# Reordered exponentials in a cross-attention loop, and a regrouped last expert stage

## The chip, the cores and the metric

One core of one Trainium2 chip runs one program: a two-layer decoder with every array in float32. The metric is the device time of one launch in microseconds (us), as the median of several launches. The kernel before takes 1028.84 us (three launches, 1027.73 to 1029.24).

## The reference, cut to what matters

The decoder works on 8 batches of 256 tokens with 128 features. The change lies in the last two of its six blocks, the second layer's cross attention and its mixture of experts:

```python
def _L1_xattn_ref(input_Q, input_K, input_V, Wq, bq, Wk, bk, Wv, bv, Wo):
    Q = _proj(input_Q, Wq, bq)          # 16 heads of 64 features
    K = _proj(input_K, Wk, bk)          # 512 positions of memory
    V = _proj(input_V, Wv, bv)
    scores = jnp.einsum('bhqd,bhkd->bhqk', Q, K) / np.sqrt(DK).astype(np.float32)
    attn = jax.nn.softmax(scores, axis=-1)
    context = jnp.einsum('bhqk,bhkd->bhqd', attn, V)
    ...
    return jnp.einsum('bse,de->bsd', context, Wo)

def _L1_ffn_ref(x, Wr, br, W1, b1, W2, b2):
    cap = max(1, int(T / E * CAPACITY_FACTOR))     # 40 slots for each of 8 experts and each batch
    ...                                            # top 2 experts of each token, buf holds the kept tokens
    h = jax.nn.relu(jnp.einsum('enc,ech->enh', buf, W1) + b1[:, None, :])
    y = jnp.einsum('enh,ehc->enc', h, W2) + b2[:, None, :]
    ...                                            # weighted sum of each token's two results
x = _layernorm(x + _L1_xattn_ref(x, ctx_1024, ctx_1024, ...), axis=-1)
x = _layernorm(x + _L1_ffn_ref(x, ...), axis=-1)
```

## The kernel before

**The loop.** Keys and values of the cross attention are computed early in the launch, kept in DRAM and loaded again. `cross_attention` then walks 64 units: a unit is one batch b and one pair of heads c (8 batches, 8 pairs). A unit has two blocks j of 128 queries, and each block two heads h. Every step i of the loop works at three units at once: it scores unit i+1, turns the weights of unit i, and multiplies the weights of unit i-1 with the values.

**The order.** The whole loop is recorded under a manual schedule. TensorE, VectorE, ScalarE and SyncE each execute their instructions in the order in which `step` issues them; an instruction whose input or buffer isn't ready holds all that stands behind it on its engine. So the order of calls in `step` is the order of work on each engine. In one step that is, by engine:

- TensorE: `score` of the next unit, block 0 and then block 1 (tile `sc`, four instructions each, L400); `product` of the former unit (tile `m`, L400); `query` of the next batch (tile `tr`, L400); the transposes of `turn(now, 0)` and then those of `turn(now, 1)` (L1508).
- ScalarE: the exponentials of `weigh(after, got, j, h)` (L1494, one 128x512 instruction each, which also sums); `keep` (L1533), which empties the product's bank; `ask` (L357), which empties the query's bank; copies of turned weights (L1605, L1613). Before the change the order is: exponential (0,0), (0,1), `keep`, `ask`, exponential (1,0), copy of `turn 0`, exponential (1,1), two copies of `turn 1`.
- VectorE: two maxima (L1487), `divide(now, 1)` (L351, L353), a copy of `turn 0` (L1604), `divide(after, 0)`.

**The buffers.** PSUM has three groups of buffers here: `sc` with 2 buffers of two banks (block 0 and block 1 of a unit's scores), `tr` with 3, `m` with 1. A buffer is handed out in turn, and its next writer waits for the last reader of the former content. A plain step takes four `tr` buffers, in this order: the query, two for `turn 0`, one for `turn 1`. With three to hand out, the one for `turn 1` is the buffer that held this step's query, so the transposes of `turn 1` wait until `ask` has read it; its other half goes to `m`, which `keep` empties. The scores of block 1 of the next unit wait until the exponentials (1,0) and (1,1) of the unit before have read theirs.

**Beside the loop.** When a batch ends (`before[1] == NQ - 1`), `finish` projects the batch on TensorE (64 matmuls into `tr`) and normalises it on VectorE. `LastExperts.route` then chooses the experts of that batch's tokens in ten pieces, which are spread over later steps; piece 0 takes a `tr` buffer and a ScalarE copy (`xr`, L1650), piece 1 a small matmul and the exponential `prob` (L1664), piece 5 a small matmul (`pos`), piece 7 the dispatch (`bufT`, L1719).

**The last stage.** `LastExperts.rest` runs behind the loop. The 8 experts run first over batches 0 to 4 (`GROUPS[0]`, 200 columns) and then over batches 5 to 7 (`GROUPS[1]`, 120 columns): `expert` makes the hidden layer (tile `sc`, then Relu on ScalarE, L1748), `result` the output (tile `tr`, then VectorE adds the bias into `val`, L1757); `settle` issues a `result` that is still pending. `back(b)` takes batch b's results back to its tokens: three transposes (L410), a ScalarE copy (L1791), and in `rest` 12 matmul instructions (L400), the sum `y` (L1799), the statistics and, one batch later, the normalised `X` (L1809) and the store. `come_back(b)` issues the transposes of batch b and then the rest of batch b-1. Before the change the transposes go to a `tr` buffer and the 12 matmuls to the one `m` buffer; two batches come back before the second group starts, three between its experts, and three behind it.

Of the kernel before, what the change touches and what calls it, by code (L numbers as in the profile page):

```python
# [21 lines left out]
P = 128  # L22
B, S, D = 8, 256, 128
SC = 512
# [119 lines left out]
class Decoder:  # L144
# [203 lines left out]
    def divide(self, u, j):  # L348
        nc, pr = self.nc, self.weights[u][j]
        rd = self.tile(self.small, [P, 2], "c_rd")  # L350
        nc.vector.reciprocal(rd, self.sums[u][j])  # L351
        for h in range(2):
            nc.vector.tensor_scalar_mul(pr[:, h, :], pr[:, h, :], rd[:, h : h + 1])  # L353
# [1088 lines left out]
    def cross_attention(self):  # L1442
# [6 lines left out]
        with self.space("ct", 2) as pool, self.space("cp", 2, space=PSUM) as ps:  # L1449
# [21 lines left out]
            def query(b, c):  # L1471

                pm = turned()
                self.mm_halves(pm[:, :S], self.wqT[:, P * c : P * (c + 1)], xTs[b])
                return pm

            def score(u):

                sc, nm = [], []
                for j in range(2):  # L1480
                    sc.append(self.tile(ps, [P, 2, SC], "sc"))
                    for h in range(2):
                        ch = slice(HD2 * h, HD2 * (h + 1))
                        self.mm(sc[j][:, h, :], queries[u][ch, P * j : P * (j + 1)], keys[u][ch, :])
                for j in range(2):
                    nm.append(self.tile(self.small, [P, 2], "c_nm"))
                    nc.vector.tensor_reduce(nm[j], sc[j], AX.X, ALU.max, negate=True)  # L1487
                prs[u] = [self.tile(self.big, [P, 2, SC], "pr", 4) for _ in range(2)]
                sums[u] = [self.tile(self.small, [P, 2], "c_sm") for _ in range(2)]
                return sc, nm  # L1490

            def weigh(u, got, j, h):
                sc, nm = got
                nc.scalar.activation(  # L1494
                    prs[u][j][:, h, :], sc[j][:, h, :], AF.Exp, bias=nm[j][:, h : h + 1],
                    accum_out=sums[u][j][:, h : h + 1],
                )
# [17 lines left out]
            def product(u):  # L1515

                b, c = u
                pc = pcs[u] = product_bank()[:, :S]
                prT = prTs.pop(u)
                for n in range(NC):  # L1520
                    for h in range(2):
                        at = P * c + HD2 * h
                        self.mm(
                            pc[HD2 * h : HD2 * (h + 1), :], vals[b][:, n, at : at + HD2], prT[:, NC * h + n, :],
                            n == 0, n == NC - 1,
                        )

            def keep(u):

                b, c = u  # L1530
                if c == 0:
                    cTs[b] = self.tile(pool, [P, NQ, S], "cT", 1)
                nc.scalar.activation(  # L1533
                    cTs[b][:, c, :], pcs.pop(u), AF.Identity, bias=self.cols[:, BV + c : BV + c + 1]
                )
# [27 lines left out]
            def step(i):  # L1563


                after, now, before = (units[k] if 0 <= k < len(units) else None for k in (i + 1, i, i - 1))
                b, c = now or (B, 0)
                got = score(after) if after and after not in early else None
                if before:
                    product(before)  # L1570
                if b + 1 < B:
                    for what in "kv":
                        self.recall(b + 1, c, what)
                    pm = query(b + 1, c)
                if c == 0 and now:
                    self.load_last_experts(b)
                if now and now not in early:
                    divide(now, 1)
                while late and i:
                    late.pop()()  # L1580
                if got:
                    weigh(after, got, 0, 0)
                    weigh(after, got, 0, 1)
                if before:
                    keep(before)
                if b + 1 < B:
                    self.ask(b + 1, c, pm)
                if before and before[1] == NQ - 1:
                    experts.early()
                    finish(before[0])  # L1590
                    routes[:] = routes[-1:] + [experts.route(before[0])]
                if now:
                    if routes and c:
                        next(routes[-1], None)
                    if len(routes) > 1:
                        for _ in range({2: 1, 5: 2}.get(c, 0)):
                            next(routes[0], None)
                    if c == 5 and b + 2 < B:
                        begin(b + 2)
                if got:  # L1600
                    weigh(after, got, 1, 0)
                if now:
                    one, two = turn(now, 0)
                    nc.vector.tensor_copy(*one)  # L1604
                    nc.scalar.copy(*two)  # L1605
                if got:
                    divide(after, 0)
                    weigh(after, got, 1, 1)
                while late:
                    late.pop()()  # L1610
                if now:
                    for what in turn(now, 1):
                        nc.scalar.copy(*what)  # L1613
# [11 lines left out]
class LastExperts:  # L1625
# [158 lines left out]
    def back(self, b):  # L1784

        nc, dec, X = self.nc, self.dec, self.X
        pt = self.tile(self.ps, [P, 4 * P], "tr", 3)[: self.CUT, : 3 * D].rearrange("p (n d) -> p n d", n=3)
        for n in range(3):
            dec.flip(pt[:, n, :], self.yT[:, b, self.CUT * n : self.CUT * (n + 1)])
        ys = self.tile(self.pool, [self.CUT, 3, D], "prT", 2)  # L1790
        nc.scalar.copy(ys, pt)  # L1791

        def rest():
            po = self.tile(self.ps, [P, SC], "m", 1)[:, : 2 * D].rearrange("p (j d) -> p j d", j=2)
            for j in range(2):
                for n in range(3):
                    dec.mm(po[:, j, :], self.backT[:, 2 * b + j, n, :], ys[:, n, :], n == 0, n == 2)
            y = self.tile(self.pool, [P, 2, D], "y")
            nc.vector.tensor_tensor(y, X[:, 2 * b : 2 * b + 2, :], po, ALU.add)  # L1799
            mv, rstd = dec.tile(dec.small, [P, NT, 2], "mv"), dec.tile(dec.small, [P, NT], "rstd")  # L1800
            for j in range(2):
                st = dec.tile(dec.small, [P, 6], "bnst")
                nc.vector.bn_stats(st, y[:, j, :])
                nc.vector.bn_aggr(mv[:, j, :], st)
            dec.rsqrt(rstd[:, :2], mv[:, :2, 1], 2, 1.0, 1e-5)

            def end():
                for j in range(2):
                    nc.vector.tensor_scalar(  # L1809
                        X[:, 2 * b + j, :], y[:, j, :], mv[:, j, 0:1], rstd[:, j : j + 1], ALU.subtract, ALU.mult  # L1810
                    )
                nc.sync.dma_start(
                    out=dec.out[b].rearrange("(j p) d -> p j d", p=P), in_=X[:, 2 * b : 2 * b + 2, :]
                )

            return end

        return rest

    def rest(self, former, route):  # L1820
        first, second = self.GROUPS
        rests, ends = [], []

        def go_on():
            ends.append(rests.pop(0)())
            if len(ends) > 1:
                ends.pop(0)()

        def come_back(b):
            rests.append(self.back(b))  # L1830
            if len(rests) > 1:
                go_on()

        self.run(first, 2)
        for piece in range(10):
            next(route, None)
            if piece in (0, 1, 3, 5):
                self.run(first)
            if piece in (1, 2, 3):
                next(former, None)  # L1840
        assert self.done == NE
        self.settle()
        for b in first[:2]:
            come_back(b)
        for n in range(NE):
            self.run(second)
            if n in (1, 3, 5):
                come_back(first[2 + n // 2])
        self.settle()
        for b in second:  # L1850
            come_back(b)
        go_on()
        ends.pop()()
# [81 lines left out]
```

## Time and profile before

| | us |
|---|---|
| median of three launches | 1028.84 |
| the profiled launch | 1028.9 |
| its span, first to last instruction | 1026.8 |
| outside the span | 2.1 |
| cross-attention loop, first to last `product` | 543.9 to 957.1 |
| last experts and ways back | about 955 to 1026.8 |
| granted TensorE clock in the loop, as a share of full speed | 1.00 |

Busy time over the whole span: TensorE 933.5 us (91%), VectorE 715.5 (70%), ScalarE 708.6 (69%), GpSimd 221.7 (22%). All times below are of the one profiled launch, counted from the start of its span. In a row of the timeline the first number is the start, the second the duration; brackets give the engine's idle time before the row and what ended it. PE is TensorE, DVE VectorE, ACT ScalarE, POOL GpSimd. A row of PE shows a matmul's modelled end; consecutive matmuls overlap, so the distance between starts tells more than the durations.

### The profile page before, as it was taken

To read this page: it belongs to the slowest core of one execution; us is meant where nothing else is said; L and a number is where in the kernel's file an instruction comes from. 1 tells how busy PE (TensorE), PEld (TensorE's weight loads), DVE (VectorE), ACT (ScalarE), POOL (GpSimd) and SP (SyncE) were. 2 spreads that over 40 slices of the span, in tenths; PEclk is the share of its full clock that TensorE was granted. 3 is DMA by queue.
4 is the path that set the end of the run, shared out by engine and by line. 5 is a ranking of instruction groups with operands and counts; after the bars stand their busy time and mean duration, and the time that the engine had idled before them with its cause. 6 is when DMAs were issued, how large, how long until landed. Compare 5 with 4: busy or idle time off the path is not lost.

```text
span 1026.8 us, 21615 instructions
## 1 busy us (share of the span) xinstructions
PE 933.5 (91%) x8141; PEld 590.9 (58%) x8141; DVE 715.5 (70%) x1726; ACT 708.6 (69%) x1682; POOL 221.7 (22%) x394
## 2 busy tenths in 40 slices
PE   6897889999888788999879999999999999999986
PEld 2343556665478455666545555555555555555886
DVE  3787765454339847677677788897979797989244
ACT  5887698787654444756557878787878787878442
POOL 1133232434225463336300000000000000010012
PEclk9998899999999989999899999999999999999998
DMA  6743565223773400000262232323232223300001
GB/s 225 232 159 93 187 201 165 91 109 147 270 233 104 161 17 25 9 6 12 14 234 80 83 104 70 101 73 114 73 99 88 94 83 104 98 8 2 2 6 37
DMA packets 84376, 103.08 MB, mean 100 GB/s; under 512 B 7200, under 2 KB 45224, under 8 KB 84272
## 3 DMA queue, kind: packets, MB, share of 16 engines
q1 hardware_dynamic: 79472, 96.68, 29.1%
q10 hardware_dynamic: 3776, 2.92, 0.9%
q0 software_dynamic: 1024, 2.10, 0.7%
q8 instruction: 64, 1.05, 0.4%
q14 instruction: 40, 0.33, 0.1%
HBM read 56.13 MB, written 45.55 MB: 99 GB/s over the span
## 4 chain that ended last, share of the span: by engine, by line
PE 58%; ACT 18%; DVE 14%; issue 4%; DMA 2%; POOL 2%; SPq 0%; POOLq 0%; DVEq 0%; ACTq 0%
PE sc L400 15%; PE bank L400 14%; PE m L400 11%; PE tr L400 9%; ACT pr L1494 5%; PE tr L410 3%; PE po L400 2%; PE tr L1508 2%; ACT prT L1605 2%; DVE c_nm L1487 1%; ACT cT L1533 1%; DVE nm L1385 1%; PE bank L410 1%; DVE ys L597 1%; DVE pr L353 1%
## 5 line engine op out<-in xcount | busy, mean ns | idle before, releaser
L1494 ACT ACTIVATE pr<-sc,c_nm 128x512 f32<-128x512 f32 x248 | 170.4, 690 | 39.9 <-DVE c_nm L1487 39.9
L1487 DVE TENSOR_REDUCE c_nm<-sc 128x2 f32<-128x1024 f32 x124 | 148.1, 1219 | 3.6 <-PE sc L400 2.0
L400 PE MATMUL sc<-kT,qT 64*128 64x512 f32 x512 | 142.5, 635 | 8.2 <-ACT pr L1494 6.9
L400 PE MATMUL m<-prT,val 128*64 128x256 f32 x1024 | 124.7, 386 | 1.9 <-ACT prT L1613 1.9
L353 DVE TENSOR_SCALAR pr<-pr,c_rd 128x512 f32<-128x512 f32 x256 | 115.1, 492 | 4.6
L400 PEld LDWEIGHTS m<-prT,val 128*64 128x64 f32 x1024 | 67.9, 137 | 77.3 <-ACT prT L1613 48.2
L1508 PE MATMUL tr<-cst,pr 64*128 64x64 f32 x1536 | 87.9, 229 | 7.6 <-ACT qT L357 5.1
L1508 PEld LDWEIGHTS tr<-cst,pr 64*128 64x128 f32 x1536 | 74.0, 139 | 30.5 <-DVE pr L353 8.8
L400 PE MATMUL bank<-wvT,ctxT 128*128 128x512 f32 x128 | 69.3, 624 | 10.5 <-DMA wvT<-in_wvT_dram 9.1
L400 PEld LDWEIGHTS sc<-kT,qT 64*128 64x128 f32 x512 | 41.0, 190 | 59.8 <-ACT pr L1494 56.1
L400 PE MATMUL bank<-ctxT,wkT 128*128 128x512 f32 x128 | 70.9, 637 | 3.2 <-ACT stage L565 1.7
L415 POOL TENSOR_SCALAR rsq<-mv 128x2 f32<-128x2 f32 (+2 forms) x57 | 13.1, 230 | 276.0 <-DVE mv L587 129.4
L1604 DVE COPY prT<-tr 128x512 f32<-128x512 f32 x64 | 43.9, 686 | 24.7 <-PE tr L1508 24.6
L1393 ACT ACTIVATE s<-sc,nm 128x128 f32<-128x128 f32 x128 | 36.6, 374 | 30.2 <-DVE s L1390 25.8
L1605 ACT COPY prT<-tr 128x512 f32<-128x512 f32 x64 | 37.6, 588 | 24.5 <-PE tr L1508 24.5
L565 ACT ACTIVATE stage<-bank,cols 128x512 f32<-128x512 f32 x57 | 39.3, 689 | 21.2 <-PE bank L400 14.7
L535 ACT COPY sT<-tr 128x512 f32<-128x512 f32 x58 | 33.5, 593 | 29.4 <-PE tr L410 29.1
L569 ACT COPY stage<-bank 128x512 f32<-128x512 f32 x58 | 33.8, 584 | 27.5 <-PE bank L400 13.3
L1385 DVE TENSOR_REDUCE nm<-sc 128x8 f32<-128x1024 f32 x32 | 39.0, 1218 | 18.9 <-PE sc L400 18.7
L1494 ACT ACTIVATION_READ_ACCUMULATOR pr<-sc,c_nm 128x1 f32 x248 | 50.3, 203 | 0.0
L416 POOL TENSOR_TENSOR rstd<-rsq,mhalf 128x2 f32<-128x2 f32 (+2 forms) x57 | 49.2, 864 | 4.8
L1508 PE MATMUL m<-cst,pr 64*128 64x64 f32 x512 | 44.7, 228 | 0.0
(366 smaller groups left out, 2031.4 us busy)
## 6 DMA issues: line engine op xcount, KB each, us to landing
mv<-stage SPq DMA_DIRECT2D x64, 256.0 KB, 2.2
mk<-stage SPq DMA_DIRECT2D x64, 256.0 KB, 2.1
kT<-mk SPq DMA_DIRECT2D x64, 256.0 KB, 2.7
val<-mv SPq DMA_DIRECT2D x64, 256.0 KB, 3.0
sorted_x<-zero SPq DMA_DIRECT2D x8, 1024.0 KB, 6.3
w<-in_m_w_dram SPq DMA_DIRECT2D x23, 256.0 KB, 2.9
f_w<-in_f_w_dram SPq DMA_DIRECT2D x16, 256.0 KB, 3.9
ctxN<-in_ctx_dram SPq DMA_DIRECT2D x8, 256.0 KB, 3.8
```

The lines of the kernel that those rows point to most:

```text
L353: nc.vector.tensor_scalar_mul(pr[:, h, :], pr[:, h, :], rd[:, h : h + 1])
L400: self.nc.tensor.matmul(out, lhsT=lhsT, rhs=rhs, start=start, stop=stop)
L410: self.nc.tensor.transpose(out, in_, self.ident)
L416: self.nc.gpsimd.tensor_tensor(out, t[:, :n], self.mhalf[:, :n], ALU.pow)
L565: nc.scalar.activation(t, pm, AF.Identity, bias=bias)
L1385: nc.vector.tensor_reduce(nm, sc, AX.X, ALU.max, negate=True)
L1393: nc.scalar.activation(s[:, 1, v, :], sc[:, 1, v, :], AF.Exp, bias=nm[:, 4 + v : 5 + v])
L1487: nc.vector.tensor_reduce(nm[j], sc[j], AX.X, ALU.max, negate=True)
L1494: nc.scalar.activation(prs[u][j][:, h, :], sc[j][:, h, :], AF.Exp, bias=nm[j][:, h : h + 1], accum_out=sums[u][j][:, h : h + 1],)
L1508: self.nc.tensor.transpose(pt[:, n, :], prs[u][j][own, n // NC, P * (n % NC) : P * (n % NC + 1)], self.ident[own, own])
L1604: nc.vector.tensor_copy(*one)
L1605: nc.scalar.copy(*two)
```

## The change

It has two parts.

1. In `step`, the exponential (1,0) of the next unit is issued directly behind (0,1), ahead of `keep` and `ask`; the exponential (1,1) takes the place that (1,0) had, ahead of `turn(now, 0)` and its copies. ScalarE's order becomes: (0,0), (0,1), (1,0), `keep`, `ask`, (1,1), copy of `turn 0`, two copies of `turn 1`. The orders of TensorE and VectorE stay as they were.
2. In `LastExperts`, the transposes of `back` move to the `m` buffer and its 12 matmuls to a `tr` buffer. In `rest`, the second group of experts starts directly behind the dispatch, before any batch has come back. Batches 0 to 3 come back between its experts (behind experts 1, 3, 5 and 7), batches 4 to 7 behind it.

```diff
                 if got:
                     weigh(after, got, 0, 0)
                     weigh(after, got, 0, 1)
+                    weigh(after, got, 1, 0)
                 if before:
                     keep(before)
...
                 if got:
-                    weigh(after, got, 1, 0)
+                    weigh(after, got, 1, 1)
                 if now:
                     one, two = turn(now, 0)
                     nc.vector.tensor_copy(*one)
                     nc.scalar.copy(*two)
                 if got:
                     divide(after, 0)
-                    weigh(after, got, 1, 1)
...
     def back(self, b):
-        pt = self.tile(self.ps, [P, 4 * P], "tr", 3)[: self.CUT, : 3 * D].rearrange("p (n d) -> p n d", n=3)
+        pt = self.tile(self.ps, [P, SC], "m", 1)[: self.CUT, : 3 * D].rearrange("p (n d) -> p n d", n=3)
...
         def rest():
-            po = self.tile(self.ps, [P, SC], "m", 1)[:, : 2 * D].rearrange("p (j d) -> p j d", j=2)
+            po = self.tile(self.ps, [P, 4 * P], "tr", 3)[:, : 2 * D].rearrange("p (j d) -> p j d", j=2)
...
-        self.settle()
-        for b in first[:2]:
-            come_back(b)
+        backs = list(first)
         for n in range(NE):
             self.run(second)
-            if n in (1, 3, 5):
-                come_back(first[2 + n // 2])
+            if n in (1, 3, 5, 7):
+                come_back(backs.pop(0))
         self.settle()
-        for b in second:
+        for b in [*backs, *second]:
             come_back(b)
```

## Prediction

> **What bounds the kernel now.** I read the page first: TensorE is busy for 91% of the span, and PEclk is 9 from the loop on, so the clock is not the matter.
>
> ```profile
> PE 933.5 (91%) x8141; PEld 590.9 (58%) x8141; DVE 715.5 (70%) x1726; ACT 708.6 (69%) x1682; POOL 221.7 (22%) x394
> ```
>
> Then the chain that ended last, in order of time, over one plain step of the loop:
>
> ```profile
> 560.38 1.13 PE sc L400 x4
> 561.51 1.90 PE m L400 x16
> 563.42 0.02 issue
> 563.44 0.46 ACT cT L1533
> 563.89 0.35 issue
> 564.24 0.31 ACT pr L1494
> 564.55 0.26 issue
> 564.82 0.20 ACT pr L1494
> 565.01 0.48 ACT prT L1605
> 565.49 0.69 ACT pr L1494 x2
> 566.18 0.04 issue
> 566.22 1.13 PE sc L400 x4
> ```
>
> The reader sees a ring of 5.84 us: scores of block 1, product, `keep`, `ask` (the 0.35 of issue), exponential (1,0), a copy, exponential (1,1), and then the next scores of block 1, whose buffer that exponential empties. The distance between products is 5.83 or 5.84 in 24 steps. Then the timeline, TensorE and ScalarE:
>
> ```profile
> 564.95 1.08 PE L400 MATMUL sc<-kT,qT 64*128 64x512 f32 x4
> 566.22 1.13 PE L400 MATMUL sc<-kT,qT 64*128 64x512 f32 x4 [0.19 <-ACT pr L1494]
> ...
> 598.20 0.71 PE L1508 MATMUL tr<-cst,pr 64*128 64x64 f32 x16 [0.84 <-ACT qT L357]
> ```
>
> ```profile
> 563.44 0.47 ACT L1533 ACTIVATE cT<-m,cols 128x256 f32<-128x256 f32 x1 [0.42 <-PE m L400]
> 563.87 0.48 ACT L357 ACTIVATE qT<-tr,bq 128x256 f32<-128x256 f32 x1
> ```
>
> The ring costs TensorE only 0.19 a step, so TensorE alone would need 5.65. The third row shows a second gate: transposes wait 0.84 for `ask` (qT), since they take the buffer that held the query. The waits, over the loop:
>
> ```profile
> PE sc L400 <- ACT pr L1494: 6.9, 34, 0.4
> PE tr L1508 <- ACT qT L357: 5.1, 6, 0.9
> ```
>
> The first row is all that the reordering can win; the second is what it can make worse. Last the timeline of the way back:
>
> ```profile
> 990.65 1.60 PE L400 MATMUL m<-prT,backT 107*128 107x128 f32 x12 [0.24 <-ACT prT L1791]
> ...
> 1018.63 1.58 PE L400 MATMUL m<-prT,backT 107*128 107x128 f32 x12 [0.61 <-DVE y L1799]
> ```
>
> TensorE waits there for the copy of the turned results and, with one `m` buffer, for `y`; between the two, at 989.72 and 1011.96, it waits 0.30 and 0.22 for `val`.
>
> **Part 1, plain steps.** Nothing is added or removed; one exponential moves ahead of `keep` and `ask`, and (1,1) ahead of a copy. The old ring loses (1,0), 0.77, and the copy, 0.48: 5.84 - 1.25 = 4.59, so it no longer closes. Next late is the gate through `ask`: scores of block 0 (564.95) to their first exponential (567.41) 2.46; three exponentials instead of two, 0.68 + 0.67 + 0.67 = 2.02; `keep` 0.35 (597.32 to 597.67, no idle ahead); `ask` to the next scores of block 0 1.08 (563.87 to 564.95). Sum 5.91, against 5.84: +0.07. The reason is ScalarE's idle of 0.42 ahead of `keep`: two exponentials fitted before the product's end, the third, 0.67, sticks out. Behind a late `ask` stand the transposes, and behind them the next scores, since TensorE runs in order. Bounds: -0.19 (TensorE alone, 5.65) and +0.29 (2.60 to the first exponential as from 629.50, `keep` 0.43 as from 609.74: 2.60 + 2.02 + 0.43 + 1.08 = 6.13). I take the sum, which is made of neighbouring rows. 18 steps (24 less the 6 that hold route piece 6): +1.3, from -3.4 to +5.2.
>
> **Part 1, steps behind a projection.** VectorE is late there, the maxima end after 597.0, and TensorE already waits 0.84 for `ask` (in the last batch 0.74 for `xr`, behind `keep`). Exponentials (0,0), (0,1), `keep`, `ask` follow without idle from 595.98 to 597.67; one more between them shifts `ask`, and so TensorE, by 0.67 in full. 7 steps: +4.7. Nothing hides it; less only if the maxima came earlier, and they follow from the projection's end.
>
> [...]
>
> **Part 1, steps with route pieces 5 and 6.** First exponential to `ask` is 2.00 and 2.01 now (625.97 to 627.97, 632.10 to 634.11), with a third 2.02 + 0.35 = 2.37: +0.36, and for the second +0.22 to +0.36, as its scores reach the exponential after 2.46 or, as now, 2.60 (5.91 or 6.05 against the 5.69 of 629.50 to 635.19). I take 0.36 + 0.22 = 0.58 for both, since a wait ahead of the transposes lets VectorE catch up. 6 batches: +3.5, from 0 to +4.3.
>
> **Part 1, the rest.** In the 7 steps with a projection the wait of 0.19 goes and 3.6 us of projection cover `ask`: -1.3, at worst 0. Behind route pieces 1 and 7 waits of 0.22 go, but the next `ask` takes them back: 0; once (599.20 to 605.20) there is no dispatch to cover `ask`: +0.3 for these, from -1.3 (six times 0.22) to +2.0 (0.3 each time). In the last batch there is no `ask`, and VectorE runs without a gap, from 929.21 to 943.34: 0, between -0.6 (three waits of 0.20) and +0.6. DMA: `recall` stays where it is, and so does SyncE's queue. GpSimd has nothing to wait for anew.
>
> Sum of part 1: 1.3 + 4.7 + 3.5 - 1.3 + 0.3 = +8.5.
>
> **Part 2.** TensorE reaches the last result of the first group at 987.85. In the new order there follow: that result 1.37, eight expert pairs of 0.89 + 0.89 (14.24), four transposes of 0.33 (1.32), three times 12 matmuls of 1.34 (4.02). Sum 20.95: the last result of the second group ends at 1008.80, now 1011.53. Covers: a Relu set takes 1.11 of the 1.78 of a pair, the dispatch copy (`bufT`) starts at 987.03 and takes 0.43, and VectorE has 1.3 us gaps. If they fail, four waits as now (0.28 to 0.61, 0.4 each) cost 1.6. Behind that result, batch 3's `y` starts at 0.33 + 1.34 + 0.03 = 1.70, and four more follow. With three buffers TensorE no longer waits for `y`; VectorE is next: `y` and statistics 1.28 (1018.06 to 1019.34), `X` 0.51, so 1.79 a batch, where it was 2.18. The last `y` starts at 1008.80 + 1.70 + 4 x 1.79 = 1017.66; it was 1020.25. So -2.6, from -3.4 to -1.0; behind `y` nothing changes.
>
> [...]
>
> **The sum.** 8.5 - 2.6 = +5.9 on the profiled launch's 1028.9 is 1034.8; the median was 0.06 lower: 1034.7.
>
> **Rivals.**
> - *Larger loss.* The third exponential meets late maxima in plain steps too. For: VectorE is at 45.7 of 53.8 us in a batch, and the maximum starts just as its multiplications end. Against: a late `ask` gives VectorE time. Plain and route steps at their upper ends, no gain at the projections: 5.2 + 4.7 + 4.3 + 0.3 - 2.6 = +11.9: 1040.7.
> - *No change.* Plain and route steps absorb the third exponential. For: `ask` stands only 0.07 later against its first exponential (2.37, now 2.30). Against: the 2.00 of the route steps. 4.7 - 1.3 - 2.6 = +0.8: 1029.6.
> - *Faster.* Plain steps fall to TensorE's own 5.65, because there the transposes' buffer comes free in time: one mechanism, the gate through `ask`, decided by whether the third exponential (0.67) fits into the time ahead of `keep`. For: every wait for scores is one for (1,1). Against: idle there is 0.42. -3.4 + 4.7 - 1.3 - 1.3 - 0.6 - 2.6 = -4.5: 1024.3.
>
> **How the numbers follow.** Forecast 0.58, larger loss 0.15, no change 0.17, faster 0.10. A difference under 0.2%, 2.1 us, can hardly be told from none: the band is 1026.8 to 1030.9, and takes the rival of no change. Slower: 0.58 + 0.15, less 0.01 for the forecast's low end: 0.72; same 0.18; faster 0.10. The range leaves out the faster rival and the far half of the larger loss: 1027.5 to 1040.5. The forecast's own range is 1031 to 1038.
>
> **What would show it.** Right: waits of `sc` for the exponentials fall from 6.9 to under 1, waits of `tr` for `ask` grow from 5.1 to above 9 and appear in plain steps; projection steps near 1.5 for the former 0.84; products 5.9 apart; last-stage end 2.6 earlier against the loop's end. Wrong: products under 5.80 apart, or no wait for `ask` in plain steps; or a last stage in which TensorE waits for `y` again.

## The result, and the profile after

The changed kernel takes 1036.88 us (median of four launches, 1036.63 to 1041.46) where the kernel before took 1028.57 on the same chip: a ratio of 1.0085, with a 95% interval of 1.0062 to 1.0107. The forecast was 1034.7, with slower at 0.72. So the sign was right, but +8.3 came where +5.9 was expected, and the sum that gave the 5.9 held two large errors of opposite sign that mostly cancelled.

The profiled launch, the one with 1041.46, spent 4.5 us more than that of before ahead of the loop, in code that the change does not touch. So its span is cut into three parts, at the first and the last `product` of the loop:

| | ahead of the loop | loop | behind the loop | span |
|---|---|---|---|---|
| before | 543.93 | 411.40 | 71.5 | 1026.8 |
| after | 548.46 | 421.36 | 69.6 | 1039.4 |
| difference | +4.5 | +9.96 | -1.93 | +12.6 |

The two parts that the change touches give +8.0, close to the 8.3 between the medians. The page of the changed kernel, its first lines and the clock:

```profile
PE 930.6 (90%) x8141; PEld 603.3 (58%) x8141; DVE 714.8 (69%) x1726; ACT 700.4 (67%) x1682; POOL 222.1 (21%) x394
...
PEclk9998899999999889999899999999999999999999
```

Nothing was added: all counts are those of before, and the busy times lie within some 2%. What moved are the waits. The waits of TensorE over the loop (us in total, times, longest):

```profile
PE tr L1508 <- ACT qT L357: 22.7, 32, 1.8
...
PE tr L1508 <- ACT xr L1650: 1.6, 1, 1.6
```

The row of `sc` waiting for `pr` is gone, and the wait for `ask` is there 32 times instead of 6. The chain that ended last, in order of time (start, us, what), over one plain step:

```profile
564.94 1.24 DVE c_nm L1487
566.18 0.02 issue
566.20 0.02 ACTq L1494
566.22 0.04 issue
566.26 1.08 ACT pr L1494 x3
567.35 0.16 issue
567.51 0.87 ACT pr L1494 x3
568.38 0.37 ACT cT L1533
568.75 0.37 ACT qT L357
...
569.88 0.94 PE sc L400 x4
```

This is the new ring, and it is the one that the prediction walked: the maximum of block 0, three exponentials (566.26 to 568.38), `keep`, `ask`, the last transposes, and the next scores of block 0 at 569.88; 5.90 from step to step. TensorE's timeline has the plain pair of scores, and two steps that follow a projection (brackets: idle time before, and what ended it):

```profile
569.72 1.94 PE L400 MATMUL sc<-kT,qT 64*128 64x512 f32 x8
...
656.12 0.71 PE L1508 MATMUL tr<-cst,pr 64*128 64x64 f32 x16 [1.73 <-ACT qT L357]
657.12 3.60 PE L400 MATMUL sc<-kT,qT 64*128 64x512 f32 x8
...
767.53 0.71 PE L1508 MATMUL tr<-cst,pr 64*128 64x64 f32 x16 [1.73 <-ACT qT L357]
768.52 1.99 PE L400 MATMUL sc<-kT,qT 64*128 64x512 f32 x8
```

Two things are to be seen. First, all eight score instructions now run as one group of 1.94; before, the second block started 1.27 behind the first block's start and the product 2.33 behind it (564.95, 566.22 and 567.28), now 0.91 and 1.87. Second, both projection steps have the same pause of 1.73, yet in the first the same eight instructions take 3.60 instead of 1.99. The windows around the two pauses (stretch, its length, then busy us of PE, PEld, DVE, ACT, POOL, granted clock, DMA share, GB/s) say why:

```profile
653.95:657.36 3.41, 1.68 (x36) 1.38 (x36) 1.81 (x5) 3.41 (x12) 0.00 (x0) 1.00 0.10 38
657.36:660.77 3.41, 3.41 (x10) 1.11 (x9) 2.34 (x6) 1.57 (x4) 0.00 (x0) 0.50 0.03 5
...
763.17:766.59 3.42, 2.63 (x23) 1.43 (x19) 3.38 (x6) 1.97 (x6) 0.00 (x0) 1.00 0.49 153
766.59:770.00 3.41, 2.47 (x39) 1.80 (x39) 1.81 (x6) 3.28 (x10) 0.00 (x0) 1.00 0.03 7
770.00:773.41 3.41, 3.41 (x36) 2.01 (x34) 3.34 (x7) 2.35 (x7) 0.00 (x0) 1.00 0.44 154
```

After the first pause the granted clock is 0.50 for 3.41 us. The kernel before has no such stretch between 544 and 1021; the changed one has five in its loop, behind four of the seven projection steps and once at the loop's end. The page's PEclk row, with slices of 26 us, shows all of them as 9, which stands for 90% or more.

Last, VectorE at the end of the span:

```profile
1030.85 0.42 DVE L1799 TENSOR_TENSOR y<-X,tr 128x256 f32<-128x256 f32 x1
...
1032.13 0.57 DVE L1809 TENSOR_SCALAR X<-y,mv,rstd 128x128 f32<-128x128 f32 x2
1032.81 0.42 DVE L1799 TENSOR_TENSOR y<-X,tr 128x256 f32<-128x256 f32 x1
```

Of the last five `y` only the first waits for TensorE (0.45); the others follow every 1.96, paced by VectorE's own chain.

### The profile page after: what moved, and what is told of

It is laid out like the page before. It is cut to its first block, busy times and chain, and to the rows that moved or that the text cites. A ratio compares the mean times of both kernels' runs of the same rounds, so it can differ in the third digit from the quotient of the medians.

```text
span 1039.4 us, 21629 instructions
## 1 busy us (share of the span) xinstructions
PE 930.6 (90%) x8141; PEld 603.3 (58%) x8141; DVE 714.8 (69%) x1726; ACT 700.4 (67%) x1682; POOL 222.1 (21%) x394
## 3 DMA queue, kind: packets, MB, share of 16 engines
q8 instruction: 64, 1.05, 0.4%
## 4 chain that ended last, share of the span: by engine, by line
PE 47%; DVE 25%; ACT 19%; issue 4%; DMA 2%; POOL 2%; SPq 0%; ACTq 0%; POOLq 0%; DVEq 0%
PE bank L400 12%; PE sc L400 12%; PE tr L400 9%; ACT pr L1494 7%; DVE c_nm L1487 6%; DVE pr L353 4%; PE tr L1508 4%; PE m L400 3%; PE tr L410 3%; PE po L400 2%; DVE prT L1605 2%; ACT cT L1533 1%; ACT qT L357 1%; DVE nm L1385 1%; PE bank L410 1%
## 5 line engine op out<-in xcount | busy, mean ns | idle before, releaser
L400 PE MATMUL sc<-kT,qT 64*128 64x512 f32 x512 | 131.4, 630 | 1.4 <-ACT s L1393 1.4
L1508 PE MATMUL tr<-cst,pr 64*128 64x64 f32 x1536 | 93.4, 234 | 26.5 <-ACT qT L357 22.7
L1508 PEld LDWEIGHTS tr<-cst,pr 64*128 64x128 f32 x1536 | 76.9, 142 | 51.6 <-ACT qT L357 27.2
L400 PEld LDWEIGHTS sc<-kT,qT 64*128 64x128 f32 x512 | 49.3, 198 | 32.7 <-issue 25.5
```

The lines of the kernel that those rows point to most:

```text
L400: self.nc.tensor.matmul(out, lhsT=lhsT, rhs=rhs, start=start, stop=stop)
L1508: self.nc.tensor.transpose(pt[:, n, :], prs[u][j][own, n // NC, P * (n % NC) : P * (n % NC + 1)], self.ident[own, own])
```

## The experiments

The kernel before took 1029.21 (first four runs), 1028.6 (next three) and 1029.96 (last two) on their chips. Each profile was cut like the one above:

| | median | ratio and interval | loop | behind the loop |
|---|---|---|---|---|
| part 1 alone | 1040.87 | 1.0098 (1.0067 to 1.0129) | 421.36 | 71.5 |
| part 2 alone | 1027.66 | 0.9982 (0.9962 to 1.0003) | 411.39 | 69.6 |
| (1,0) held back at `c == 1` | 1025.13 | 0.9959 (0.9940 to 0.9979) | 411.36 | 69.6 |
| both exponentials behind `ask` | 1019.15 | 0.9896 (0.9865 to 0.9927) | 404.50 | 69.6 |
| three matmuls in the pause | 1031.19 | 1.0023 (1.0011 to 1.0036) | 414.84 | 69.6 |
| before, pause made longer | 1040.31 | 1.0124 (1.0085 to 1.0163) | 425.03 | 71.5 |
| before, pause a little longer | 1032.07 | 1.0034 (1.0015 to 1.0054) | 414.87 | 71.5 |
| one matmul in the pause | 1030.50 | 1.0004 (0.9985 to 1.0024) | 415.55 | 69.6 |
| as the fourth, `ask` moved up | 1020.61 | 0.9901 (0.9869 to 0.9934) | 405.75 | 69.6 |

What lies ahead of the loop varied from 542.2 to 548.9 between the profiled launches, without a change there. So a median is uncertain by a few us, and the columns of the loop and the end are the sharper ones.

**The two parts alone.** Part 1 alone moves both exponentials and leaves the last stage as it was:

```diff
                     weigh(after, got, 0, 1)
+                    weigh(after, got, 1, 0)
...
-                    weigh(after, got, 1, 0)
+                    weigh(after, got, 1, 1)
...
-                    weigh(after, got, 1, 1)
```

> Part 1 alone, on the kernel before. Both theories: the whole loss and more is in part 1, 1028.6 + 10.1 = about 1038.7 us, part 2 giving back 1.9 in the changed kernel. Queue theory (a late ask holds TensorE, nothing else): the last product stands 2 to 3 us later against the first than the 411.4 of before, apart from stretches at half clock. Clock theory: three to five stretches of 3.4 us at half clock inside the loop, each behind a projection step, where before had none, and 1.6 us of loss for each. If the clock were chance, they would be as frequent elsewhere in the loop.

Part 2 alone is the rest of the diff, `back` and `rest`.

> Part 2 alone. From the trace of the changed kernel: the way from the last first-group result to the last y takes 30.6 us instead of 32.6, so 1026.7 us, -1.9. If the prediction's 1.79 a batch behind the second group were right, -2.6: 1026.0. No half-clock stretch inside the loop by either theory, since the loop is that of before.

The loop took 421.36 with part 1 and 411.39 with part 2, the values of after and before; behind the loop it was the other way round, 71.5 and 69.6. So the parts add up without touching each other: part 1 costs 10.0 in these profiles, part 2 gains 1.9. In the medians the gain of part 2 is 1.55, and its interval reaches 1.0003.

**The steps behind a projection.** Two theories were left for the 10 us. Queue: the third exponential delays `ask`, TensorE waits, and that is all. Clock: the longer pause also brings the half clock, which costs again. The first test takes the early exponential away in just those steps:

```diff
-                    weigh(after, got, 1, 0)
+                    if c != 1:
+                        weigh(after, got, 1, 0)
...
+                    if c == 1:
+                        weigh(after, got, 1, 0)
                     weigh(after, got, 1, 1)
```

> The changed kernel, but in the one step a batch behind a projection (c = 1) the exponential (1,0) stays behind ask, as before. Queue theory: TensorE's wait there falls from 1.73 to about 1.0, 0.65 each in 7 steps and the last batch's, -4.6 to -5.2: about 1032.0 us, and nothing more. Clock theory: the shorter wait no longer lets the clock drop, so the half-clock stretches of the loop go as well, 1.6 us each for four: about 1026 us.

The loop fell by 10.0, to 411.36. The only half-clock stretch left in it is the one at its end. TensorE's timeline has the pause at 1.05, and behind it the scores at full clock:

```profile
651.54 0.71 PE L1508 MATMUL tr<-cst,pr 64*128 64x64 f32 x16 [1.05 <-ACT qT L357]
...
652.54 1.99 PE L400 MATMUL sc<-kT,qT 64*128 64x512 f32 x8
```

The seven steps lost 9.9 of their 10.7. Seven pauses that are 0.68 shorter make 4.8 of that at most; the queue alone cannot give it. But this edit takes away pause and clock drop together, and so the next ones move them apart.

**Work added into the pause.** The changed kernel, with matmuls whose product is overwritten unread, ahead of the transposes that wait:

```diff
-            def turn(u, j):
+            def turn(u, j, fill=0):
...
+                for _ in range(fill):
+                    self.mm(pts[0].rearrange("p n t -> p (n t)")[:, :S], self.ident, self.cst[:, :S])
...
-                    one, two = turn(now, 0)
+                    one, two = turn(now, 0, 3 if c == 1 else 0)
```

> The changed kernel with three more matmuls of 128x256 in each step that follows a projection (7 of them), put into the free transpose bank ahead of the transposes that wait for ask's queries; their products are overwritten unread, so nothing is computed differently. They add 7 x 3 matmuls of about 0.44 us of TensorE work, which lies inside the 1.73 us for which TensorE stands there now. Queue theory (the lost time is ScalarE's longer path to the queries): the time stays at 1036.9, within 1 us, since TensorE still cannot go on before the queries come. Clock theory (part of it is the half clock that follows a pause of 1.73 us): the pause that is left is about 0.4 us, no half-clock stretch is left in the loop, the three steps of 9.2 fall to 7.6 and the loop is some 6 us shorter: about 1030.6, a kernel with more work that takes less time.

It took 1031.19, 5.7 less than the changed kernel, with more work. TensorE's timeline, at the second of these steps (each of the three added matmuls is two instructions there):

```profile
651.95 1.46 PE L400 MATMUL tr<-cst 128*128 128x256 f32 x6
...
654.04 0.71 PE L1510 MATMUL tr<-cst,pr 64*128 64x64 f32 x16 [0.42 <-ACT qT L357]
...
655.04 1.99 PE L400 MATMUL sc<-kT,qT 64*128 64x512 f32 x8
```

`ask` comes no sooner: the steps are 7.6 long, as those of the changed kernel that kept the full clock, in every batch but the last (6.98). No half clock is left in the loop, nor at its end, where a line of the clock's windows cut the pause of 1.41 into 0.54 and 0.87. The loop's first step, which has no pause but gets the matmuls too, pays 1.3 for them. This is the clean separation: the same queue without the clock.

The same with one matmul in place of three:

> The changed kernel with one more 128x256 matmul instead of three ahead of the waiting transposes, in the seven steps that follow a projection: TensorE's pause there falls from 1.73 to about 1.3 us, and the queries come no sooner. Queue theory: 1036.9 as the changed kernel. Clock theory, with the limit between 1.2 and 1.5 us of idle in one window of the clock's grid: no half clock behind any of these pauses, steps of 7.6, and about 1031, the same as with three matmuls. If a pause of 1.3 is still enough, some steps of 9.2 are left and the time lies between the two.

A row of TensorE's timeline:

```profile
650.41 0.71 PE L1510 MATMUL tr<-cst,pr 64*128 64x64 f32 x16 [1.28 <-ACT qT L357]
```

And the window of the clock's grid that holds this pause, with the one behind it:

```profile
647.47:650.88 3.41, 2.12 (x26) 1.22 (x23) 2.04 (x4) 3.36 (x10) 0.00 (x0) 1.00 0.30 115
650.88:654.29 3.41, 3.41 (x41) 1.99 (x39) 3.15 (x6) 2.21 (x6) 0.00 (x0) 1.00 0.02 5
```

The pause is 1.28. Five of that length lie whole in one such window, and the next window is at 1.00 each time. The time was 1030.50, as with three: 0.45 us of useless work (the pause's 1.73 less 1.28), put where TensorE stands anyway, takes away all that the clock cost in those steps (a stretch at the loop's end, worth 1.5, stayed).

**The pause made longer in the kernel before.** No exponential is moved; ScalarE gets instructions whose result nobody reads:

```diff
+                if c == 1 and before:
+                    held = self.tile(pool, [P, P], "held", 1)
+                    for _ in range(3):
+                        nc.scalar.activation(held, self.wqT[:, :P], AF.Identity, bias=self.bq2[:, 0:1])
                 if before:
                     keep(before)
```

> The kernel before, with three ScalarE instructions of 128x128 (about 0.25 us each, their result unread) ahead of keep in the seven steps that follow a projection. No exponential is moved: ask and the queries only come about 0.8 us later, so TensorE's pause there grows from 0.85 to about 1.65 us. Queue theory: 7 x 0.8 = 5.6 at most, 1034 to 1035. Clock theory: that, and a half-clock stretch of 3.41 us behind three or four of the seven pauses at about 1.6 us each: 1039 to 1041, with stretches in the loop that the kernel before has not.

It took 1040.31, and its loop 425.03, 13.6 more than before. The three instructions cost 1.15 a step, not the 0.8 that was expected, so the pause was 2.0 and the queue's share 8.1 rather than 5.6; the time alone then tells the theories apart only weakly (1036.7 against some 1041.6). The rows do it: four of the seven steps lost exactly that 1.15 or 1.16, two of the others 2.38 and 2.42, one 2.20, and these three are the ones followed by half clock. A fourth stretch stands at the loop's end (1.4), and the loop's first step, where the edit falls too, lost 0.35. TensorE's timeline at the first of the three:

```profile
652.27 1.12 PE L1508 MATMUL tr<-cst,pr 64*128 64x64 f32 x16 [2.01 <-ACT qT L357]
653.93 2.80 PE L400 MATMUL sc<-kT,qT 64*128 64x512 f32 x8
```

The windows there:

```profile
648.72:652.13 3.41, 1.54 (x13) 0.71 (x9) 2.15 (x5) 3.18 (x10) 0.00 (x0) 1.00 0.38 133
652.13:655.54 3.41, 3.27 (x35) 2.65 (x37) 1.65 (x4) 3.15 (x9) 0.00 (x0) 0.50 0.03 7
```

The half clock comes with the pause, then, and does not need the change of order. With one such instruction:

> The same with one ScalarE instruction instead of three: the pause grows to about 1.1 to 1.2 us. Queue theory: 7 x 0.3 = 2, 1031. Clock theory has the same unless the drop begins below 1.2 us; pauses of 1.05 us brought none in two earlier runs, so no half-clock stretch in the loop and 1031 here would put the limit between 1.2 and 1.7.

Pauses of 1.14 (1.02 in the last batch), all seven steps longer by 0.29 or 0.30, none followed by half clock. The loop is 3.5 longer than before's: 2.0 from these steps, and 1.5 from a stretch at the loop's very end, behind a pause of 1.85 that the kernel before has too, but cut in two by the clock's windows there. The median, 1032.07, is 3.5 above before's.

**Both exponentials behind `ask`.** The other half of part 1 without the early one: `keep` and `ask` come right behind block 0 again, and (1,1) stays ahead of the copies.

```diff
                     weigh(after, got, 0, 1)
-                    weigh(after, got, 1, 0)
...
                 if got:
+                    weigh(after, got, 1, 0)
                     weigh(after, got, 1, 1)
```

> The changed kernel with the exponential (1,0) back behind ask, and (1,1) directly behind it, still ahead of the copies. Queue theory: ask is as early as before, the scores of block 1 find their buffer free, so the two blocks follow each other in 1.9 us (changed kernel) instead of 2.35 (before): plain steps between 5.4 and 5.75, waits of TensorE for the exponentials near 0, waits for ask back to 0.85 in projection steps. 60 steps at -0.1 to -0.3: 6 to 15 us below the loop of before, and part 2's 1.9: 1012 to 1021 us. Rival: VectorE's 45.7 of 53.8 us a batch, with its waits, becomes the bound, and less than 4 us come out: 1023 to 1027.

1019.15: faster than both kernels, by 1.0% against before. The loop is 6.9 shorter than before's. TensorE's waits over the loop are now:

```profile
PE m L400 <- ACT prT L1613: 12.1, 35, 1.9
PE tr L1508 <- ACT qT L357: 6.3, 6, 1.1
```

The scores never wait, `ask` is early, and the next gate is the product, which waits 0.30 for the last copy; plain steps are 5.74 apart. The rival, VectorE as the bound with less than 4 us to gain, is out. So what was worth moving in the old order was (1,1) from behind the copy, not (1,0) from behind `ask`: from this version to the changed kernel, which differs in (1,0) alone, the loop grows by 16.9, of which the half clock has 7.8 (see below).

Last, the wait of 1.05 that is left behind a projection was attacked, by moving `ask` ahead of (0,1) and `keep` in those steps:

```diff
                     weigh(after, got, 0, 0)
+                if b + 1 < B and c == 1:
+                    self.ask(b + 1, c, pm)
+                if got:
                     weigh(after, got, 0, 1)
                 if before:
                     keep(before)
-                if b + 1 < B:
+                if b + 1 < B and c != 1:
                     self.ask(b + 1, c, pm)
```

> The version with both exponentials of the second block behind ask (1019.15), with ask moved ahead of the second exponential and of keep in the steps that follow a projection. TensorE's wait of 1.05 for the queries there falls to about 0 (six steps). If that wait is what these steps cost, they fall from 7.06 to about 6.0 and the time to 1013. If ScalarE's chain from the first exponential to the last copy sets them (5.2 us from 646.32 to 651.5, the next product at 651.60), its length is unchanged, the wait comes back ahead of the next product and the time stays within 1 us of 1019.

TensorE's timeline in one of these steps:

```profile
650.46 0.27 PE L1508 MATMUL tr<-cst,pr 64*128 64x64 f32 x1 [0.59 <-ACT xr L1653]
...
653.26 1.95 PE L400 MATMUL m<-prT,val 128*64 128x256 f32 x16 [0.32 <-ACT prT L1616]
```

The steps stayed at 7.07 (before this edit 7.06), and the time did not fall: 1020.61 against 1019.15, whose launches overlap. The loop grew by 1.25, of which 1.04 lies in its first step, where the edit falls too. Of the 1.05, 0.59 came back as a wait for `xr`, the next reader of that pool, and 0.32 as a wait of the product. So it is ScalarE's chain that sets these steps, as the second of the two expectations had it, and TensorE's wait only shows where it is met.

## Why the prediction was right, and where it was not

By its own steps, in us over the loop, measured as distances between products in the changed kernel less those of before:

| steps | predicted | measured |
|---|---|---|
| 18 plain | +1.3 | +1.0 |
| 7 behind a projection | +4.7 | +10.7 (4.3 without half clock, by the one matmul in the pause) |
| 12 with route pieces 5 and 6 | +3.5 | -0.5 |
| 7 with a projection | -1.3 | -1.4 |
| 6 with route pieces 1 and 7 | +0.3 | -2.8 |
| 7 with `begin` and route pieces 4, 8, 9 | none | +1.6 |
| 6 in the last batch | 0 | +1.4 (0.0 without half clock) |
| part 1 | +8.5 | +10.0 |
| part 2 | -2.6 | -1.9 |
| both | +5.9 | +8.0 |

- The mechanism was right: the ring through (1,1) opened, the ring through `ask` closed at 5.90 (5.91 predicted; link by link 2.44, 2.01, 0.35 and 1.10, where 2.46, 2.02, 0.35 and 1.08 were summed), the scores' wait went from 6.9 to none, and behind a projection a whole exponential was added: 0.65 per step where the clock stayed up, 0.67 predicted. TensorE held its order: before, the scores start at 599.20 behind the transposes of 598.20 that had waited 0.84, and after, at 657.12 behind those of 656.12 that had waited 1.73; so nothing filled the pause. The rivals of the larger loss and of the faster kernel both rested on plain steps that moved by 0.3 or 0.2; they moved by 0.06.
- **The clock step failed.** "PEclk is 9 from the loop on, so the clock is not the matter" was true of the loop of the kernel before, with pauses of 0.85 (only the page's last slice, the tail, shows 8). The change doubled the pause, and the prediction never asked what a longer pause does to the clock. That is worth 6.4 in the projection steps (10.7 less 4.3). Another 1.4 comes from the stretch in the loop's last step, 7.8 in all, but there no pause grew: it was 1.85 before, cut by a line of the clock's windows, and is 1.41 after, whole in one of them.
- **The waits of the scores were read too small.** "The ring costs TensorE only 0.19 a step" took the bracket at its word. From block 0's first score to the product is 2.33 in the plain steps of before and 1.87 after: 0.46 was being lost, and TensorE alone would need 5.38, not 5.65. The version with both exponentials behind `ask` says the same: its product stands 2.23 behind the first score, 0.37 more than 1.87, and 5.74 less that is 5.37. The brackets hid it: block 1 starts 1.27 behind block 0 and, without a wait, 0.91, which makes 0.36 of the 0.46; but the row of block 0 (564.95) lasts 1.08, so the bracket shows only 0.19 of that. Where another gate stood close behind (plain steps) this changed nothing; where none did it was a gain that the sum lacks. With route pieces 1 and 7 the steps fell by 0.45 to 0.48, the whole of it; "the next `ask` takes them back: 0" was wrong. With pieces 5 and 6 they moved by -0.13 and +0.06 where +0.36 and +0.22 were taken; that it was these waits there too is argued, and no run tried it.
- **A term was left out.** The seven steps with `begin` got none, and no reason was given. They cost +1.6; what sets them was not tried.
- So without the half clock part 1 comes to 10.0 - 7.8 = +2.2 and not +8.5, and with part 2 to +0.3, which is no change. The two kernels with the pause filled agree. With one matmul the loop is 4.2 longer than before's, 0.6 of it in the first two steps, which pay for the matmuls, and 1.5 in the stretch at the end; with three it is 3.4 longer, 1.5 of it in the first two steps. About +2 is left in both.
- **The total was in part luck.** The sum of part 1 was 6.3 too high for a full clock (4.0 of it with route pieces 5 and 6, 3.1 with 1 and 7), and the half clock, for which it had no term, added 7.8. With a full clock throughout, by this account, its rival of no change would have come true.
- **Part 2** had the right path and one term too small. From the point named, the last result of the second group ended 20.95 later, as summed, and the first `y` came 1.70 behind it, as summed; but the five `y` are 1.96 apart, not 1.79, since from `X` to the next `y` it takes 0.68 (1032.13 to 1032.81) and not the 0.51 that was taken. Four times that is the 0.7 that was missed. VectorE was the bound, as said: TensorE's 12 matmuls were already 1.67 apart (1023.45, 1025.12, 1026.79), and the `y` stayed 1.96 apart. The 3.4 at the far end of the part's range is shown by no run; part 2 alone and both parts together gave 1.9 (71.5 less 69.6).

Open: why the maxima behind a projection come as late as they do was not tried, and ScalarE's chain in those steps starts there.

## What to carry to other kernels

When an edit lengthens a pause of TensorE, price the clock as well as the queue: look at the granted clock in windows of a few us, since the page's slices of 26 us showed none of the five stretches of 3.41, and if the pause can't be shortened, try harmless matmuls in it (here one took the time from 1036.88 to 1030.50). Take the true cost of a wait from the distance between starts, against a place where the same group runs without a wait, not from the idle time in brackets. And when a ring has two links that could be moved, move each alone: here the one that helped was worth 6.9 us in the loop, and the other cost 16.9, nearly half of it by the clock.

## What the hardware showed that was not expected

The half-clock stretches lie on a fixed grid. In the changed kernel's loop those five start at 657.36, 711.97, 875.81, 930.42 and 964.56: 16, 48, 16 and 10 times 3.413 us apart (the first and the last are 307.20 apart, a ninetieth of which is 3.413), and each is 3.41 long. In most of the pauses counted below, what follows goes with how much of the pause falls into one window of that grid. The pause that ended at 656.12 lay whole in the window from 653.95; the equal one that ended at 767.53 was cut by the line at 766.59 into 0.79 and 0.94, and nothing followed. Counting all pauses behind projections in the changed kernel, in part 1 alone and in the kernel before with the longer pause, 21 in all: the 11 that were followed by half clock had 1.61 to 2.00 of idle time in one window; of the 10 others eight had at most 1.44, and two had 1.58 and 1.72. In the eight profiles whose pauses there were 1.36 or shorter none was followed. By these 21 the limit, as an estimate, lies between 1.44 and 1.61 us of idle time in a window of 3.41, but it is not sharp in idle time alone: beside the 1.58 and the 1.72 that brought nothing, at the loop's end one window with 1.86 (in the last experiment) was followed by full clock and one with 1.23 (with one matmul in the pause) by half. The first of these held 1.33 us of the product and 0.23 of transposes, the second 1.65 of transposes. Whether the kind of work counts beside its time was not shown, since no run varied it, and what else counts is open.

The price of one stretch behind a projection was about 1.6 us in the changed kernel (9.2 less 7.6), a little under half of 3.41, and 1.1 to 1.3 in the kernel before with the longer pause. The same pause of 1.73 cost that at 656.12 and nothing more at 767.53, by where it fell. The grid's place against the start of the span differed between the profiles (its first line lay 0.2 to 2.4 us behind it), but against the loop's first product it lay nearly the same in all eleven (a line 2.85 to 3.16 us behind it), and in every one a half-clock stretch ended 0.2 to 0.6 us ahead of that product (the eight scores there took 3.23 to 3.54, where 1.94 to 1.99 is their length at full clock). So which pauses were hit followed from the lengths of the loop's own steps: in the changed kernel and in part 1 alone it was the same four of seven. With the longer pause in the kernel before it was the second, the fourth and the seventh, where those two had the second, the third, the sixth and the seventh; whether an edit ahead of the loop would shift them was not tried.
